# A column block of the attention weights is turned by VectorE and DMAs instead of TensorE

## The chip, the cores and the metric

The kernel runs on one core of a Trainium2 chip. The metric is device time in microseconds, from the program's start to its end. A core has a matrix engine (TensorE, PE in the profile; its weight loads are PEld), a vector engine (VectorE, DVE), an engine for activations (ScalarE, ACT), a general engine (GpSimd, POOL) and one that mostly issues DMAs (SyncE, SP). Each runs its own queue of instructions in order; semaphores make one wait for another. Results of TensorE go to a small memory, PSUM, and are copied from there to the main on-chip memory, SBUF, by VectorE or ScalarE.

## The reference

There are 32 graphs of 512 nodes with 64 features each and one normalized adjacency matrix for all. Four layers follow each other, each with a layer norm before it and a residual sum behind it. The change concerns the fourth, which takes most of the time:

```python
def gat_layer(x, graph, W, b):
    h = x @ W
    s = jnp.einsum('bnd,bmd->bnm', h, h) * graph
    s = jnp.where(s == 0.0, NEG_INF, s)
    a = jax.nn.softmax(s, axis=2)
    return jnp.einsum('bnm,bmd->bnd', a, h) + b
heads = jax.vmap(lambda W, b: gat_layer(flow_x, graph, W, b))(Wh, bh)   # 8 heads, 128 wide
x = jax.nn.leaky_relu(cat, negative_slope=0.01)                          # heads side by side
out = gat_layer(x, graph, W_out, b_out)                                  # 64 wide
return jax.nn.leaky_relu(out, negative_slope=0.01)
```

All is float32. The softmax is taken along rows, and the product with the values sums over the columns, so the weights have to be transposed between the two: TensorE sums over the partition axis, which holds rows after the softmax and has to hold columns for the product.

## The kernel before

The first three layers take the first 470 us or so. Then comes the attention stage, `run`, which the change touches. Its piece of work is a **unit** (`Pair`): two heads of one graph (`Heads`, 128 units) or the output layer of two graphs (`Out`, 16 units). A unit's weights p_att hold, for each of its two members k, 512 rows as four groups r of 128 partitions, by 512 columns as four blocks j of 128.

The stage goes in **slots**, four to a unit, and the order in each slot is written out by hand (`slot(k)`, in a manual schedule) for TensorE, VectorE and ScalarE. What a unit does is given by its offset from its first slot:

- offset -1 to 2: the scores of row group r (L387), 0 to 3: the softmax's front (`soft`): s_att on VectorE (L373), the exponentials p_att on ScalarE (L366);
- offset TR = 5 to 8: the transposes of block j (L400), 16 of them for each block, into two PSUM buffers pt_ps for the lower and upper half of the rows. ScalarE copies one half to pt_att (L406), VectorE the other (L408);
- offset VA = 6 to 9: the values av of block j (L415), which accumulate over the four blocks;
- offset 5, on VectorE at the end of the slot: `recips`, the reciprocal of the row sums and a small transpose; SyncE then writes them to DRAM (rec_row, L430) and reads them back as rows (recb, L435);
- offset END = 9: `normalize` (L444), av times recb, and after it the projection of the heads (y_ps, L527), cat (L535), and leaky (L312).

Units overlap. The slot in which one unit has offset 9 is the slot in which the next has offset 5, so in VectorE's order of that slot the normalize of one unit stands ahead of recips of the next: s_att twice, normalize, the pt_att copy, recips.

Every fourth head unit (a new graph) has one more chain: VectorE makes hn at the end of one slot (L475 to L479), GpSimd makes hs of it in two operations (L484), TensorE transposes hs in the next slot (hx_ps, L291), and ScalarE copies that to hx, from which the scores' operand g comes (g_ps, L509). In the nine units that belong to two graphs, eight slots also hold a product gT_ps (L566) for the output layer.

Pools matter in three places: pt_ps, y_ps, g_ps, hx_ps and gT_ps share three PSUM buffers, the scores have two, p_att has two. GpSimd and SyncE are not in the manual schedule; their orders follow that of the program.

Of the kernel before, what the change touches and what calls it, by code (L numbers as in the profile page):

```python
# [8 lines left out]
F32 = mybir.dt.float32  # L9
# [5 lines left out]
P = 128  # L15
# [7 lines left out]
def fast_form(  # L23
# [25 lines left out]
    nc = tc.nc  # L49
    B, N, F = x.shape  # L50
    C = N // P
    H, _, D = w_heads.shape
    G = min(8, B)
    NG = B // G
    F2 = 2 * F

    const = ctx.enter_context(tc.tile_pool(name="const", bufs=1))
    xpool = ctx.enter_context(tc.tile_pool(name="xpool", bufs=1))
# [30 lines left out]
    def load_blockdiag(src, name):  # L89
        t = setup.tile([P, F2], F32, name=name)  # L90
        nc.vector.memset(t, 0.0)
        for k in range(2):
            nc.gpsimd.dma_start(t[k * F : (k + 1) * F, k * F : (k + 1) * F], src)
        return t
# [34 lines left out]

    wgT2 = setup.tile([P, F2], F32, name="wgT2")  # L130
    bh = const.tile([P, H], F32, name="bh")
# [74 lines left out]
    def halves(k):  # L206
        return slice(k * F, (k + 1) * F)
# [8 lines left out]
    def acc(name, shape):  # L216
        return acc_of[0].tile(shape, F32, name=name, tag=acc_of[1])
# [22 lines left out]
    def gat_weights():  # L240
        pw = acc("wgT_ps", [P, F2])
        nc.tensor.transpose(pw, wg2, ident)
        nc.scalar.copy(wgT2, pw)
        pa = acc("wa_ps", [P, 2])
        nc.tensor.matmul(pa, lhsT=wg2, rhs=a12, start=True, stop=True)
        wa = setup.tile([P, 2], F32, name="wa")
        nc.scalar.copy(wa, pa)
        nc.vector.memset(wa2, 0.0)
        for k in range(2):
            nc.vector.tensor_copy(wa2[halves(k), k : k + 1], wa[halves(k), 1:2])  # L250
        nc.vector.memset(wa1, 1.0)
        size = tiny.tile([P, 2], F32, name="size")
        nc.vector.scalar_tensor_tensor(size, wa, -1.0, wa, op0=OP.mult, op1=OP.max)

        pz = acc("size_ps", [P, 2])
        nc.tensor.matmul(pz, lhsT=wa1, rhs=size, start=True, stop=True)
        nc.vector.tensor_scalar(
            sound[:, :2], pz, 2 * E_MAX, None, op0=OP.is_le
        )
        nc.vector.tensor_scalar(wa1, wa1, wa[:, 0:1], None, op0=OP.mult)  # L260
# [39 lines left out]
    TR = C + 1  # L300
# [13 lines left out]
    class Pair:  # L314
# [4 lines left out]

        def begin(self):
            self.p = pbuf.tile([P, 2, C, N], F32, name="p_att")
            self.sum = tiny.tile([P, 2, C], F32, name="sum_att")
            self.negmax = tiny.tile([P, 2, C], F32, name="negmax")
            self.pts = {}
# [55 lines left out]
        def scores(self, r):  # L382
# [3 lines left out]
            for k in range(2):  # L386
# [2 lines left out]
                    start=True, stop=True,  # L389
                )  # L390

        def transpose(self, j):
            pt = pbuf.tile([P, 2, N], F32, name="pt_att", bufs=2)
            self.pts[j] = [pt[:, k] for k in range(2)]

            ps = [ps_m.tile([P, 2, C, F], F32, name="pt_ps", tag="m") for half in range(2)]
            for k in range(2):
                for r in range(C):
                    for half in range(2):
                        nc.tensor.transpose(  # L400
                            ps[half][:, k, r],
                            self.p[halves(half), k, r, j * P : (j + 1) * P],
                            ident[halves(half), halves(half)],
                        )
            pth = pt.rearrange("p k (r half q) -> p k r half q", r=C, half=2)
            nc.scalar.copy(pth[:, :, :, 0, :], ps[0])  # L406

            return lambda: nc.vector.tensor_copy(pth[:, :, :, 1, :], ps[1])  # L408

# [218 lines left out]
    with (  # L628
# [92 lines left out]
        def project(terms, tag):  # L721
            p = ps_o.tile([P, C, 2, F], F32, name=tag, tag="po")
            for c in range(C):
                for i, (t, w) in enumerate(terms):
                    nc.tensor.matmul(  # L725
                        p[:, c],
                        lhsT=t[:, c * P : (c + 1) * P],
                        rhs=w,
                        start=(i == 0),
                        stop=(i == len(terms) - 1),  # L730
                    )
            return p
# [104 lines left out]
        def slot(k):  # L837
# [50 lines left out]
            if l1:  # L888
                po = project([(nt1, wl2[0])], "po1a")
                z = work.tile([P, C, F2], F32, name="z")  # L890
                nc.scalar.activation(z, po.rearrange("p c b f -> p c (b f)"), AF.Relu)
# [60 lines left out]
    wk = ctx.enter_context(tc.tile_pool(name="work_b", bufs=2))  # L952
# [9 lines left out]
    def run(units, products):  # L962
        units = units + [None] * 4

        def at(k, off, span=C):

            for u in range(len(units)):
                if units[u] and 0 <= k - u * C - off < span:
                    yield units[u], k - u * C - off

        exps = []

        def led_in(k):
            for u, j in at(k, -3 * C, 3 * C + END + 5):
                if u.leads(j - 3 * C):
                    yield u, j - 3 * C

        def slot(k):
            for u, r in at(k, -1):
                u.scores(r)  # L980

            led = list(led_in(k))
            for u, off in led:
                u.row_halves(off)

            while exps:
                exps.pop(0)()

            copies = []

            def transposes():
                for u, j in at(k, TR):
                    copies.append(u.transpose(j))

            if not led:
                transposes()
            for u, j in at(k, VA):
                u.values(j)  # L1000
            for u, j in at(k, VA - 1, 1):
                u.make_v()
            for n, u in products:
                u.product(k - n * C)
            for u, j in at(k, -3 * C, 3 * C):
                u.prep_pe(j - 2 * C)
            if led:
                transposes()
            for u, j in at(k, END, 5):
                u.end_pe(j)  # L1010

            def mid():
                for u, j in at(k, END, 1):
                    u.normalize()

            now = list(at(k, 0))
            for u, r in now:
                exps.append(u.soft(r, mid))
            if not list(led_in(k + 1)):
                while exps:  # L1020
                    exps.pop(0)()
            if not now:
                mid()
            for copy in copies:
                copy()
            for u, j in at(k, END, 5):
                u.end_late(j)
            for u, j in at(k, TR, 1):
                u.recips()
            for u, j in at(k, -3 * C, 3 * C):  # L1030
                u.prep_late(j - 2 * C)

        with tc.manual_schedule(
            engines={
                mybir.EngineType.PE,
                mybir.EngineType.DVE,
                mybir.EngineType.Activation,
            }
        ):
            for k in range(-3 * C, len(units) * C):  # L1040
                slot(k)
# [56 lines left out]
def general_form(  # L1098
# [27 lines left out]
    NG = B // G  # L1126
    F2 = 2 * F

# [18 lines left out]
    def load_blockdiag(src, name):  # L1147
        t = const.tile([P, F2], F32, name=name)
        nc.vector.memset(t, 0.0)
        for k in range(2):  # L1150
            nc.gpsimd.dma_start(t[k * F : (k + 1) * F, k * F : (k + 1) * F], src)
        return t
# [462 lines left out]
def gnn_stack_kernel(tc: tile.TileContext, *args: bass.AP):  # L1615
    nc = tc.nc
    with tc.tile_pool(name="flag", bufs=1) as pool:
        again = pool.tile([1, 1], mybir.dt.int32, name="again")
        fast_form(tc, *args, again)
        with tc.If(nc.values_load(again[0:1, 0:1])):  # L1620
            general_form(tc, *args)
# [35 lines left out]
```

## Time and profile before

| | before |
|---|---|
| time, median of 3 runs | 2357.64 us (2357.25 to 2358.01) |
| span of the profiled run | 2359.7 us |
| one of the exponentials, L366 | 723 ns, 1152 of them |
| one s_att, L373 | 680 ns, 1152 |
| pt_att copy on VectorE, L408 / ScalarE, L406 | 687 / 581 ns, 576 each |
| one transpose instruction, L400 | 226 ns, 9216, overlapping |
| DMAs in the attention stage | 24 GB/s, all from SyncE |
| DMAs issued by GpSimd | only in the first 15 us |

Instructions overlap in an engine's pipeline, so a mean times a count is more than the engine's busy time. The chain of waits goes back from the last instruction, at each step to what released it; its shares say which engine the end waited for. A group's idle time names who ended it. In the lists in order of time, the first number is the start in microseconds from the span's start, the second the duration.

### The profile page before, as it was taken

Reading aid. Unit: us, or ns where it says so; the run is one execution under the profiler, and the core shown is the slowest. Engines: PE = TensorE matmul, PEld = TensorE weight load, DVE = VectorE, ACT = ScalarE, POOL = GpSimd, SP = SyncE. Lnnn points to the kernel's source line nnn. Section 1 sums busy time; section 2 is a strip of 40 time slices with the busy share of each in tenths; the row PEclk is TensorE's granted clock in tenths of the full one; section 3 lists DMA queues with packets and bytes.
Section 4 is the critical chain, followed back from the end, with each engine's and each line's share of the span. In section 5 each row is a group of like instructions: output and inputs, shape, how many; then the busy total and the mean of one; then the engine's idle time right before and its main releaser. Section 6 shows DMA issues by size and latency. Waiting matters only on the chain.

```text
span 2359.7 us, 46961 instructions
## 1 busy us (share of the span) xinstructions
PE 2259.6 (96%) x17786; PEld 1107.3 (47%) x17786; DVE 1792.1 (76%) x4350; ACT 1583.2 (67%) x3660; POOL 68.0 (3%) x104
## 2 busy tenths in 40 slices
PE   7999999689999999999999999999999999999997
PEld 4677777634444444444444444444444444444443
DVE  5788878577777777777777777777777787878776
ACT  3444443277777777777777777777777777778775
POOL 2000000000000000000000000000000000000000
PEclk9999999589999999999999999999999999999999
DMA  3000000000000000000000000000000000000001
GB/s 106 1 1 1 1 1 1 0 15 24 20 28 21 27 24 24 28 20 28 22 26 24 24 24 24 24 24 24 24 24 26 22 29 19 24 19 24 20 24 38
DMA packets 44059, 51.89 MB, mean 22 GB/s; under 512 B 15864, under 2 KB 25248, under 8 KB 43696
## 3 DMA queue, kind: packets, MB, share of 16 engines
q1 hardware_dynamic: 43312, 48.60, 6.6%
q8 instruction: 142, 2.33, 0.4%
q0 software_dynamic: 512, 0.20, 0.1%
q14 instruction: 93, 0.76, 0.1%
HBM read 43.98 MB, written 4.78 MB: 21 GB/s over the span
## 4 chain that ended last, share of the span: by engine, by line
PE 89%; DVE 6%; POOL 2%; ACT 1%; issue 1%; DMA 1%; SPq 0%; POOLq 0%; DVEq 0%; ACTq 0%
PE s_ps L387 23%; PE av L415 22%; PE pt_ps L400 13%; PE nt_ps L706 7%; PE acc L789 6%; PE gT_ps L566 5%; PE y_ps L527 5%; PE g_ps L509 2%; DVE pt_att L408 2%; POOL hs L484 2%; PE po L725 1%; PE hx_ps L291 1%; PE e_ps L753 1%; PE po1a L725 1%; PE wh L725 1%
## 5 line engine op out<-in xcount | busy, mean ns | idle before, releaser
L366 ACT ACTIVATE p_att<-s_att,negmax 128x512 f32<-128x512 f32 x1152 | 827.6, 723 | 0.0
L373 DVE CUSTOM_DVE_ANT_0 s_att<-s_ps,flow_neg 128x512 f32<-128x512 f32 x1152 | 739.9, 680 | 5.3 <-PE s_ps L387 5.2
L408 DVE COPY pt_att<-pt_ps 128x512 f32<-128x512 f32 x576 | 395.6, 687 | 281.0 <-PE pt_ps L400 223.7
L387 PE MATMUL s_ps<-hx,g 64*128 64x512 f32 x2048 | 571.0, 636 | 5.8 <-DVE negmax L373 5.1
L415 PE MATMUL av<-pt_att,hn 128*64 128x512 f32 x2048 | 552.4, 618 | 0.0
L400 PEld LDWEIGHTS pt_ps<-ident,p_att 64*128 64x128 f32 x9216 | 373.6, 138 | 374.1 <-issue 227.7
L406 ACT COPY pt_att<-pt_ps 128x512 f32<-128x512 f32 x576 | 334.6, 581 | 156.6 <-PE pt_ps L400 150.7
L400 PE MATMUL pt_ps<-ident,p_att 64*128 64x64 f32 x9216 | 415.2, 226 | 2.3 <-ACT pt_att L406 0.8
L535 ACT ACTIVATE cat<-y_ps,bh 128x512 f32<-128x512 f32 x256 | 162.0, 684 | 168.4 <-PE y_ps L527 168.4
L387 PEld LDWEIGHTS s_ps<-hx,g 64*128 64x128 f32 x2048 | 156.5, 188 | 245.7 <-DVE negmax L373 178.3
L366 ACT ACTIVATION_READ_ACCUMULATOR p_att<-s_att,negmax 128x1 f32 x1152 | 224.5, 195 | 0.0
L444 DVE TENSOR_TENSOR o_att<-av,recb 128x512 f32<-128x512 f32 x144 | 99.6, 691 | 140.5 <-PE av L415 140.5
L415 PEld LDWEIGHTS av<-pt_att,hn 128*64 128x64 f32 x2048 | 101.4, 135 | 156.7 <-PE s_ps L387 86.4
L312 DVE SCALAR_TENSOR_TENSOR cat<-cat 128x1024 f32<-128x1024 f32 x128 | 155.6, 1215 | 0.0
L789 PE MATMUL acc<-v,s 128*128 128x65 f32 x1024 | 136.5, 301 | 10.3 <-DVE s L779 10.3
L789 PEld LDWEIGHTS acc<-v,s 128*128 128x128 f32 x1024 | 134.8, 217 | 13.5 <-issue 12.3
L527 PE MATMUL y_ps<-o_att,wh_sb 64*128 64x512 f32 x512 | 131.7, 591 | 0.0
L566 PE MATMUL gT_ps<-cat,wo_sb 128*64 128x512 f32 x512 | 131.7, 593 | 0.0
L521 ACT COPY g<-g_ps 128x512 f32<-128x512 f32 x128 | 68.7, 589 | 84.8 <-PE g_ps L509 84.8
L706 PE MATMUL nt_ps<-adj_t,hn 128*128 128x512 f32 x256 | 115.9, 596 | 0.8 <-DVE hn L670 0.8
L373 DVE DVE_READ_ACCUMULATOR2_ANT negmax<- 128x1 f32 x1152 | 95.6, 83 | 0.0
L387 PE MATMUL s_ps<-gs 64*128 64x512 f32 x256 | 72.3, 641 | 24.2 <-DVE gs L584 24.2
(169 smaller groups left out, 1603.1 us busy)
## 6 DMA issues: line engine op xcount, KB each, us to landing
recb<-rec_row SPq DMA_DIRECT2D x288, 128.0 KB
rec_row<-rect SPq DMA_DIRECT2D x576, 1.0 KB
out_dram<-y SPq DMA_DIRECT2D x32, 128.0 KB
x<-in_x_dram SPq DMA_DIRECT2D x3, 1024.0 KB
x<-in_x_dram SPq DMA_DIRECT2D x4, 256.0 KB
adj_raw<-in_adj_dram SPq DMA_DIRECT2D x1, 1024.0 KB
wh_sb<-in_L_gnn_Wh_dram SPq DMA_DIRECT2D x2, 256.0 KB
wo_sb<-in_L_gnn_W_out_dram SPq DMA_DIRECT2D x1, 256.0 KB
```

What stands on the lines that cost most here:

```text
L366: nc.scalar.activation(self.p[:, k, r, :], ns[:, k], AF.Exp, bias=self.negmax[:, k, r : r + 1], scale=-1.0, accum_out=self.sum[:, k, r : r ...
L373: nc.vector.tensor_tensor_reduce(out=ns[:, k], in0=ps[:, k], in1=flow_neg[:, r], scale=-1.0, scalar=BIG, op0=OP.add, op1=OP.min, accum_out ...
L387: nc.tensor.matmul(ps[:, k], lhsT=g[halves(k), r * P : (r + 1) * P], rhs=x[halves(k), :], start=True, stop=True,)
L400: nc.tensor.transpose(ps[half][:, k, r], self.p[halves(half), k, r, j * P : (j + 1) * P], ident[halves(half), halves(half)],)
L406: nc.scalar.copy(pth[:, :, :, 0, :], ps[0])
L408: return lambda: nc.vector.tensor_copy(pth[:, :, :, 1, :], ps[1])
L415: nc.tensor.matmul(self.av[halves(k), :], lhsT=self.v(k, j), rhs=pt[k], start=(j == 0), stop=(j == C - 1),)
L527: nc.tensor.matmul(ps, lhsT=wh_sb[halves(k), h, :], rhs=self.o[halves(k), :], start=True, stop=True,)
L535: nc.scalar.activation(self.cat[:, k], pss[k], AF.Identity, bias=bh[:, h : h + 1], scale=1.0)
L566: nc.tensor.matmul(self.gps[halves(k), :], lhsT=wo_sb[:, h, :], rhs=Heads.cat[b + k, h], start=(h == 0), stop=(h == H - 1),)
L706: nc.tensor.matmul(p, lhsT=lhs(k), rhs=adj_t[:, k, :], start=(k == 0), stop=(k == C - 1))
L789: nc.tensor.matmul(acc[:, r], lhsT=self.s[k][j // 2][:, j % 2, r * P : (r + 1) * P], rhs=self.v[:, k, j], start=(j == 0), stop=(j == C - 1),)
```

## The change

The transpose of the last of the four column blocks leaves TensorE. At offset 5, after `recips` and so behind VectorE's other work of that slot, the new `route` has VectorE transpose the 32 by 32 pieces of block 3 inside their quarter of the partitions, with one instruction for each of the two members. The pieces then lie in the right orientation but, except for those on the diagonal, in the wrong quarter of the partitions. Sixteen DMAs of 32 partitions by 1 KB move them from `turn` to `turned`: the four on the diagonal from SyncE, the other twelve from GpSimd. The values of block 3 at offset 9 read `turned`. Both new buffers are double.

With the blocks that stay on TensorE, the second copy goes to ScalarE for blocks 0 and 2 and stays on VectorE for block 1, so ScalarE now has five of the six copies of a unit. It is meant to take work from TensorE and copies from VectorE.

```diff
+        def route(self, j):
+            t = wk.tile([P, Q, 2, C, 32], F32, name="turn")
+            for k in range(2):
+                nc.vector.transpose(
+                    t[:, :, k].rearrange("p a r i -> p r a i"),
+                    self.p[:, k, :, j * P : (j + 1) * P].rearrange(
+                        "p r (a i) -> p r a i", i=32
+                    ),
+                )
+            pt = wk.tile([P, Q, 2, C, 32], F32, name="turned")
+            for b in range(Q):
+                for a in range(Q):
+                    (nc.sync if a == b else nc.gpsimd).dma_start(
+                        pt[a * 32 : (a + 1) * 32, b], t[b * 32 : (b + 1) * 32, a]
+                    )
+            self.pts[j] = [pt[:, :, k].rearrange("p b r q -> p r b q") for k in range(2)]
...
             nc.scalar.copy(pth[:, :, :, 0, :], ps[0])
+            if j != 1:
+                nc.scalar.copy(pth[:, :, :, 1, :], ps[1])
+                return None
 
             return lambda: nc.vector.tensor_copy(pth[:, :, :, 1, :], ps[1])
...
             def transposes():
-                for u, j in at(k, TR):
+                for u, j in at(k, TR, C - 1):
                     copies.append(u.transpose(j))
...
             for copy in copies:
-                copy()
+                if copy:
+                    copy()
...
             for u, j in at(k, TR, 1):
                 u.recips()
+                u.route(C - 1)
```

## The prediction

> **What bounds the kernel now.** I read the shares first, then the chain of waits, then busy time by stretch, then one stretch in order of time.
>
> ```profile
> PE 2259.6 (96%) x17786; PEld 1107.3 (47%) x17786; DVE 1792.1 (76%) x4350; ACT 1583.2 (67%) x3660; POOL 68.0 (3%) x104
> ...
> PE 89%; DVE 6%; POOL 2%; ACT 1%; issue 1%; DMA 1%; SPq 0%; POOLq 0%; DVEq 0%; ACTq 0%
> PE s_ps L387 23%; PE av L415 22%; PE pt_ps L400 13%; PE nt_ps L706 7%; PE acc L789 6%; PE gT_ps L566 5%; PE y_ps L527 5%; PE g_ps L509 2%; DVE pt_att L408 2%; POOL hs L484 2%; PE po L725 1%; PE hx_ps L291 1%; PE e_ps L753 1%; PE po1a L725 1%; PE wh L725 1%
> ```
>
> TensorE sets the time, and the transposes (L400) are 13% of the chain: 0.13 x 2359.7 / 576 column blocks = 0.53 us a block. The one GpSimd item is hs, 2%, although POOL is busy for 3%: the chain passes through it.
>
> ```profile
> 1000.00:1500.00 500.00, 488.58 (x4116) 210.29 (x4116) 385.27 (x975) 374.83 (x899) 10.65 (x18) 1.00 0.08 25
> ```
>
> That is the busy time by stretch (length, then PE, PEld, DVE, ACT, POOL, clock, DMA share, GB/s) in the attention stage: PE 98%, DVE 77%, ACT 75%.
>
> The issues of rec_row on SyncE come once a unit, so their starts give the units' periods. From 1485.58 us they are 13.3, 11.3, 14.9, 14.7, 13.7, 13.3, 11.9 and 12.2 us; hs returns every 116.5 us (1440.62 to 1557.10), so a cycle is nine units and the ninth takes 11.3. Sixteen cycles are 1864 us. The two units of 13.3 are those with hs in them. The chain through one of them:
>
> ```profile
> 1550.73 1.01 PE av L415 x4
> 1551.74 1.06 PE s_ps L387 x4
> 1552.80 0.86 PE y_ps L527 x4
> 1553.66 1.01 PE av L415 x4
> 1554.67 0.69 PE pt_ps L400 x16
> ...
> 1556.14 0.34 DVE hn L475
> ...
> 1556.51 0.43 DVE hn L476
> ...
> 1557.10 1.20 POOL hs L484 x2
> ...
> 1558.34 0.65 PE hx_ps L291 x4
> ```
>
> From the end of a unit's last values (1551.74) to hx_ps is 6.60 us, and TensorE waits about 0.5 us for hs; from hx_ps to the next unit's last values (ending at 1565.02) it is 6.7.
>
> **What the Trainium skill says.** "DMA: Bandwidth & Descriptors", section "Anatomy of one DMA": a GpSimd DMA costs about 2.0 us plus bytes / 436e3, mostly the wait for the write's receipt. Before has such DMAs only in its start, from HBM beside the big loads, where they landed after 4.6 to 8.1 us; no SBUF to SBUF one is in the trace. "SBUF — State Buffer", section "Who interferes with whom": a VectorE instruction outside the two-port modes with at most one SBUF input does not hold up GpSimd. The stage's copies (687 ns for 512 elements from PSUM) and leaky (1215 for 1024) run at about one element a cycle, so I charge no starvation of descriptors. "TensorE: Matmul & The Clock Gate", Part 1: a whole idle window of about 3.4 us halves the clock. The slices of before agree in kind: 0.5 from 405 to 485 us, where TensorE has gaps of 5 to 10 us.
>
> **The change part by part.**
>
> TensorE: 16 transposes a unit go, 0.53 us. Times 144 units: -77 us if nothing else comes to bind.
>
> ScalarE: two more copies (blocks 0 and 2), one fewer (block 3): +0.58 us a unit (581 ns, L406). From 374.83/500 x 12.95 = 9.7 us a unit to 10.3, against 12.4 that TensorE would need: off the path. I charge nothing; the work hiding it is TensorE's.
>
> VectorE: three of four copies go (3 x 687 = 2.06 us), two transposes of 128x512 come. Before shows only STREAM_TRANSPOSE of 128x32 at 211 ns; other operations of 512 elements take 680 to 690. Bounds 0.68 and, at half that rate, 1.3; I take 0.72, paced 0.65. In total VectorE does less, but the new work stands behind normalize and recips of its slot, and normalize waits for the previous unit's last values.
>
> GpSimd: 12 DMAs a unit. Start-up shows the cost of one:
>
> ```profile
> L93 POOL DMA_DIRECT2D ws<-n_L_gnn_weight_self_dram x2 | 1.1, 543 | 0.0
> ...
> L117 POOL DMA_DIRECT2D b_out<-in_L_gnn_b_out_dram x2 | 1.1, 533 | 0.0
> ...
> L104 POOL DMA_DIRECT2D bias_b<-in_L_gnn_bias_dram x1 | 0.8, 756 | 0.4 <-issue 0.4
> L126 POOL DMA_DIRECT2D bh_raw<-in_L_gnn_bh_dram x1 | 0.5, 542 | 0.0
> ```
>
> 64 rows, 64 rows of one element, 128 rows, 8 rows: fixed cost, little with rows. I take 0.53; bounds 0.50 and 0.756. Twelve take 6.4 us. In the built program each waits for the landing of the one eight before it (8 x 0.53 = 4.2 us earlier), which costs nothing at a landing of 2.5 us. Behind them in GpSimd's queue stand the two hs operations (in every fourth head unit the order is 12 DMAs, hs, hs), and for hs waits hx_ps, in order on TensorE.
>
> SyncE: 4 more issues, 0.32 us each by rec_row's pace (1.29 for four), ahead of recb. recb starts 1.3 us later and has some 6 us in hand; the four land before GpSimd's twelve. Nothing. The 0.5 MB a unit over 12 us is 43 GB/s beside 24 now, and q1 takes 6.6% of the DMA engines for 48.6 MB: no bound.
>
> **The new loop.** Time 0 is the end of a unit's last values. normalize, reciprocal and the small transpose: 1.05 (their records after 1551.74, less the copy of block 0 that leaves VectorE). Two transposes: to 2.4. First DMA at 2.5, the twelfth starts at 2.5 + 11 x 0.53 = 8.3. Landing 2.5 after its start (bounds 2.0, the skill's fixed cost, and 4.6): 10.8. TensorE's waits for twelve semaphores 0.2 (my guess), values 1.08: the period can't be under 12.1 us.
>
> **hs.** The twelfth is issued at 8.9, hs ends at 10.1, hx_ps starts at 10.15 instead of 6.60: +3.55, less the 0.53 removed: +3.0.
>
> By cycle: two hs units +6.0; the short ones 11.3, 11.3, 11.9, 12.2 go to 12.1: +1.7; the three long ones (14.9, 14.7, 13.7) stay bound by TensorE and gain 0.53 each: -1.6. Sum +6.1, times 16: +98 us. The idle gap at hx_ps is about 4.0 us; a free-running window of 3.4 fits whole into it in some (4.0 - 3.4)/3.4, about one in five, and costs some 2 us: 32 x 0.2 x 2 = +12. 2357.6 + 98 + 12 = **2468 us**.
>
> **Rivals.**
> - *TensorE stays the bound, all DMAs hidden*: 2357.6 - 77 = 2281. For it: 98% busy, three slots between the turn and its use. Against: twelve issues at the start-up price leave hs late whatever the landing. It needs issues under about 0.35 us, which no row shows. 0.07; half hidden, around 2330, another 0.04.
> - *The gain and the two waits cancel*: 2358, with issues of about 0.4 us. 0.02.
> - *GpSimd is dearer than start-up shows*. At 0.756 an issue: loop 2.5 + 11 x 0.756 + 2.5 + 1.3 = 14.6 for all seven units without hs (+12.7 a cycle), hs units +5.7 each: +24 x 16 = 385, 2740. At 0.53 but landing 4.6: the ninth waits 0.4, loop 14.6, hs units +3.4: +19 x 16 = 310, 2668. For it: 4.6 is the least landing measured. Against: those read HBM beside megabyte loads. 0.24, most of it below 2680.
> - *VectorE's longer slot holds scores up*: scores of the slot after next need the score buffer read by then. s_att ends near 3.95, TensorE asks at 3.6: 0.4 us, which lies inside the waits above. Slow transposes (1.3) would shift route, hs and loop by 1.2: two hs units +2.4, four short ones +4.8, times 16, +115: 2580, inside the range.
> - *ScalarE becomes the bound*: 10.3 of 12 us; 0.01.
>
> **How the numbers follow.** Forecast (both waits on GpSimd, 2400 to 2560) 0.62; dearer GpSimd 0.25 with the ScalarE case; cancelled 0.02; faster 0.11. The range, 2365 to 2680, leaves out the faster cases (0.11) and the top of the dear one (some 0.07). Faster 0.11, same 0.02, slower 0.87.
>
> **What would show it.** Right: the chain's share of GpSimd and DMA grows from 3% to above 15%, PE's busy share falls to about 88% (2259.6 - 77 of 2468), TensorE's waits before av name DMAs in the short units, before hx_ps name hs at some 4 us, pt_ps falls to 6912 instructions. Wrong if: DMA_DIRECT2D on POOL is well under 0.4 us, hs runs within 1 us of hn, or units without hs are shorter than 11 us.

## The result, and the profile after

The changed kernel takes 2578.64 us (median of 4 runs, 2577.62 to 2579.96), the kernel before 2357.82 in the same comparison: ratio 1.0928, 95% interval 1.0913 to 1.0944, 221 us slower. The forecast had the direction and both waits, and half of the amount: 2468 us, so 110 us of the 221.

Shares and costliest groups of the changed kernel's page (busy us, mean ns of one | idle time of the engine just before them, and what ended most of it):

```profile
PE 2262.9 (88%) x15482; PEld 1042.4 (40%) x15482; DVE 1714.4 (67%) x4206; ACT 1645.2 (64%) x3804; POOL 914.1 (35%) x1832
...
L407 POOL DMA_DIRECT2D turned<-turn x1728 | 845.4, 497 | 1354.6 <-issue 654.0
L390 PE MATMUL s_ps<-hx,g 64*128 64x512 f32 x2048 | 609.2, 674 | 45.2 <-DVE negmax L376 44.5
...
L398 DVE STREAM_TRANSPOSE turn<-p_att 128x512 f32<-128x512 f32 x288 | 187.9, 690 | 52.6 <-issue 46.9
...
L292 PE MATMUL hx_ps<-ident,hs 128*128 128x128 f32 x128 | 29.7, 373 | 123.3 <-POOL hs L507 122.5
...
turned<-turn POOLq DMA_DIRECT2D x1728, 32.0 KB, 2.1
```

All engines but GpSimd have lost share, so the time is in waits. The last line's 2.1 us is the median from issue to landing. TensorE's waits in the attention stage, 490 to 2560 us (total us, times, longest):

```profile
PE hx_ps L292 <- POOL hs L507: 122.5, 31, 6.7
PE av L438 <- DMA turned<-turn: 53.4, 42, 3.6
PE s_ps L390 <- DVE negmax L376: 44.1, 76, 1.8
```

The same view of before, over its attention stage, has none for `turned` and for the other two:

```profile
PE hx_ps L291 <- POOL hs L484: 14.3, 31, 0.8
PE s_ps L387 <- DVE negmax L373: 4.8, 13, 0.4
```

These three waits therefore grew by 201 us, of 213 by which TensorE's idle time grew (span less PE busy: 2575.7 - 2262.9 = 312.8, against 2359.7 - 2259.6 = 100.1).

The surprise is in PE's busy time. With 77 us of transposes gone it should be 2183; it is 2263. The attention stage as one stretch, of before (columns as in the prediction):

```profile
490.00:2345.00 1855.00, 1809.33 (x15296) 778.63 (x15292) 1421.88 (x3586) 1388.41 (x3325) 36.69 (x62) 1.00 0.08 24
```

And of the changed kernel:

```profile
490.00:2560.00 2070.00, 1814.28 (x13017) 714.79 (x13014) 1346.68 (x3447) 1451.15 (x3470) 882.79 (x1790) 0.96 0.21 58
```

The clock fell from 1.00 to 0.96: fewer instructions, slower in the mean. Over the span the mean clock went from 0.981 to 0.948. As an estimate that counts idle time too, what the clock takes away is (1 - clock) times the span: 0.052 x 2575.7 = 134 us against 0.019 x 2359.7 = 45, so 89 us more. The span's difference adds up as -77 (transposes) + 80 (slower matmuls) + 213 (idle) = 216.

By units (starts of rec_row), a typical cycle went from 13.3 11.3 14.9 14.7 13.7 13.3 11.9 12.2 11.3 (116.6) to **18.1 12.1 14.2 14.2 13.1 18.2 12.0 12.7 12.0** (126.6): +10 x 16 = 160 us. The other 61 are stray longer units. A unit with hs, in order of time (start, length, [idle before]):

```profile
1541.97 1.08 PE L438 MATMUL av<-turned,hn 128*64 128x512 f32 x4
...
1544.50 1.30 DVE L398 STREAM_TRANSPOSE turn<-p_att 128x512 f32<-128x512 f32 x2 [0.36 <-issue]
...
1546.34 5.85 POOL L407 DMA_DIRECT2D turned<-turn  x12 [7.23 <-DMA rec_row<-rect]
...
1547.97 0.43 DVE L499 SCALAR_TENSOR_TENSOR hn<-hn,rstd 128x256 f32<-128x256 f32 x1
...
1552.21 1.19 POOL L507 TENSOR_TENSOR hs<-hn,root_d 128x256 f32<-128x256 f32 x2
1553.46 1.11 PE L292 MATMUL hx_ps<-ident,hs 128*128 128x128 f32 x4 [3.76 <-POOL hs L507]
1554.50 2.08 PE L390 MATMUL s_ps<-hx,g 64*128 64x512 f32 x4
1556.37 1.92 PE L532 MATMUL g_ps<-hx,m 64*128 64x512 f32 x4
```

hn has been ready since 1548.40 (1547.97 + 0.43), hs starts the moment the twelfth issue ends, and hx_ps starts 10.5 us after the last values' end (1542.98). Then the matmuls run at half speed: the scores take 2.08 us for the 1.13 they take at full clock, g_ps 1.92 for 1.02. With hx_ps itself (1.11 for 0.65) that is 2.3 us.

### The profile page after: what moved, and what is told of

It is laid out like the page before. It is cut to its first block, busy times and chain, and to the rows that moved or that the text cites. A ratio compares the mean times of both kernels' runs of the same rounds, so it can differ in the third digit from the quotient of the medians.

```text
span 2575.7 us, 46612 instructions
## 1 busy us (share of the span) xinstructions
PE 2262.9 (88%) x15482; PEld 1042.4 (40%) x15482; DVE 1714.4 (67%) x4206; ACT 1645.2 (64%) x3804; POOL 914.1 (35%) x1832
## 3 DMA queue, kind: packets, MB, share of 16 engines
q8 instruction: 127, 2.08, 0.4%
## 5 line engine op out<-in xcount | busy, mean ns | idle before, releaser
L407 POOL DMA_DIRECT2D turned<-turn x1728 | 845.4, 497 | 1354.6 <-issue 654.0
L390 PE MATMUL s_ps<-hx,g 64*128 64x512 f32 x2048 | 609.2, 674 | 45.2 <-DVE negmax L376 44.5
L438 PE MATMUL av<-pt_att,hn 128*64 128x512 f32 x1536 | 419.9, 625 | 0.0
L420 PEld LDWEIGHTS pt_ps<-ident,p_att 64*128 64x128 f32 x6912 | 277.5, 139 | 270.5 <-issue 187.0
L426 ACT COPY pt_att<-pt_ps 128x512 f32<-128x512 f32 x432 | 251.1, 581 | 143.2 <-PE pt_ps L420 143.0
L420 PE MATMUL pt_ps<-ident,p_att 64*128 64x64 f32 x6912 | 299.4, 225 | 1.2 <-ACT pt_att L426 0.6
L398 DVE STREAM_TRANSPOSE turn<-p_att 128x512 f32<-128x512 f32 x288 | 187.9, 690 | 52.6 <-issue 46.9
L438 PE MATMUL av<-turned,hn 128*64 128x512 f32 x512 | 141.6, 628 | 44.1 <-DMA turned<-turn 38.7
L428 ACT COPY pt_att<-pt_ps 128x512 f32<-128x512 f32 x288 | 170.9, 593 | 0.0
L438 PEld LDWEIGHTS av<-pt_att,hn 128*64 128x64 f32 x1536 | 77.2, 137 | 210.1 <-issue 108.1
L812 PEld LDWEIGHTS acc<-v,s 128*128 128x128 f32 x1024 | 134.9, 217 | 13.5 <-issue 12.3
L292 PE MATMUL hx_ps<-ident,hs 128*128 128x128 f32 x128 | 29.7, 373 | 123.3 <-POOL hs L507 122.5
```

What stands on the lines that cost most here:

```text
L390: nc.tensor.matmul(ps[:, k], lhsT=g[halves(k), r * P : (r + 1) * P], rhs=x[halves(k), :], start=True, stop=True,)
L398: nc.vector.transpose(t[:, :, k].rearrange("p a r i -> p r a i"), self.p[:, k, :, j * P : (j + 1) * P].rearrange("p r (a i) -> p r a i", i ...
L407: (nc.sync if a == b else nc.gpsimd).dma_start(pt[a * 32 : (a + 1) * 32, b], t[b * 32 : (b + 1) * 32, a])
L420: nc.tensor.transpose(ps[half][:, k, r], self.p[halves(half), k, r, j * P : (j + 1) * P], ident[halves(half), halves(half)],)
L428: nc.scalar.copy(pth[:, :, :, 1, :], ps[1])
L438: nc.tensor.matmul(self.av[halves(k), :], lhsT=self.v(k, j), rhs=pt[k], start=(j == 0), stop=(j == C - 1),)
```

## The experiments

Before, in these comparisons, took 2359 to 2360 us (medians). Each kernel starts from the changed one unless its edit says otherwise. e3 and e4 leave the move between partitions out of what the values read.

### The two waits, one at a time

**e1**: hs on VectorE, so nothing of TensorE's stands behind the issues.

```diff
-                    nc.gpsimd.tensor_tensor(
+                    nc.vector.tensor_tensor(
```

> The change, with hs made by VectorE (L507: nc.vector instead of nc.gpsimd) so that it no longer stands behind the twelve DMAs in GpSimd's queue. Theory (the queue in front of hs is the main cost, and the half clock follows from that gap): TensorE's wait before hx_ps falls from 3.8 us to under 1, the units with hs fall from 18.1 to about 13, the clock of the stage goes back to about 0.99; 32 x 5 = 160 us less, 2420 (2380 to 2450). Rival (the wait for the DMAs' landing in every unit is the main cost): only the hx_ps wait goes, 32 x 2 = 60 us or less, 2520 or more.

Measured: 2413.52 us, ratio 1.0234 (1.0217 to 1.0251), 165 us less than the changed kernel. TensorE's waits in its attention stage:

```profile
PE av L438 <- DMA turned<-turn: 57.5, 41, 4.0
...
PE hx_ps L292 <- DVE hs L507: 1.6, 6, 0.4
```

The waits for hs are gone, the hs units are mostly back at 13.2 to 13.7, the mean clock is 0.975. The short units mostly stay at 11.7 to 12.7, and the waits before av for `turned` stay too (53.4 us in the changed kernel).

**e3**: all DMAs issued, but the values read `turn`, so none waits for a landing.

```diff
-            self.pts[j] = [pt[:, :, k].rearrange(...) for k in range(2)]
+            self.pts[j] = [t[:, :, k].rearrange(...) for k in range(2)]
```

> The change, with the sixteen DMAs issued as before but the values of block 3 reading turn instead of turned, so that TensorE doesn't wait for any landing (this leaves the move between partitions out of the result). Theory: hs units stay at 17 to 18 us, the short units fall from 12.0 to about 11: 4 a cycle x 1 us x 16 = 64, with the stray late landings up to 90: 2500 (2480 to 2540). Rival (landing is the main cost): below 2420.

Measured: 2509.73 us, 1.0641 (1.0623 to 1.0658). The hs units take 19.0 us at the median (18.2 in the changed kernel), and the clock is the lowest with e10's, 0.943.

**e4**: the same without the 16 DMAs.

```diff
-            pt = wk.tile(...)
-            for b in range(Q): ...dma_start(...)
```

> The change without its sixteen DMAs: VectorE turns block 3, and the values of block 3 read turn (this leaves the move between partitions out of the result). What is left is TensorE's saving, the new copies and VectorE's longer slot. Theory: TensorE stays the bound and 144 x 0.53 = 77 us are gained, less up to 0.4 us for scores behind VectorE in the short units (4 of 9 of 144, 25 us): 2290 (2275 to 2310). Rival (ScalarE's copies or VectorE's slot cost as much as they save): 2340 or more.

Measured: 2285.16 us, 0.9693 (0.9676 to 0.9709). Its typical cycle is 12.7 10.8 14.2 14.2 13.1 12.7 11.4 12.2 10.8. Its page:

```profile
PE 2176.7 (95%) x15482; PEld 1012.3 (44%) x15482; DVE 1700.8 (75%) x4206; ACT 1644.4 (72%) x3804; POOL 67.9 (3%) x104
```

This is the gain that was hoped for: 74 us of 77, with the new transposes and copies in place. So the whole loss is in the DMAs. Added to e4, DMAs that nobody reads cost 2510 - 2285 = 225 us, some 200 of them in the hs units (32 x 6.3, from 12.7 to 19.0), so mostly by the queue in front of hs; reading what they bring costs 69 more. From the other side, e1 puts the loop at 2414 - 2285 = 128 us and hs at 165. The two overlap, so neither split is a property of one wait alone; the queue is the larger part either way.

### The clock

**e2**: two unneeded matmuls into hx_ps ahead of its transposes, so that half of TensorE's gap is filled.

```diff
+                for _ in range(2):
+                    nc.tensor.matmul(pt, lhsT=ident, rhs=urow, start=True, stop=True)
```

> The change, with two matmuls of ident by urow (128x512 each) into hx_ps just ahead of the transposes of hs, whose results are overwritten: 2 us of added TensorE work in the gap of 3.8 us in each of 32 units, hs as late as before. Theory (the gap halves the clock afterwards, and that costs about 2.3 us a time): no idle window is long enough, scores and g after hx_ps go back from 2.08 and 1.92 to 1.13 and 1.02 us, 32 x 2.3 = 70 us less: 2505 (2490 to 2530). Rival (the slow matmuls come from something else, such as the DMAs' traffic): same or slower, 2575 to 2640.

Measured: 2539.77 us, 1.0758 (1.0735 to 1.0781): 39 us less, for more work, where 70 had been expected. Mean clock 0.966. The filling didn't always help. Two units with the same wait, in order of time:

```profile
1145.92 0.66 PE L521 MATMUL hx_ps<-ident,hs 128*128 128x128 f32 x4 [1.85 <-POOL hs L507]
1146.51 1.13 PE L390 MATMUL s_ps<-hx,g 64*128 64x512 f32 x4
...
1273.40 0.66 PE L521 MATMUL hx_ps<-ident,hs 128*128 128x128 f32 x4 [1.85 <-POOL hs L507]
1273.99 2.02 PE L390 MATMUL s_ps<-hx,g 64*128 64x512 f32 x4
```

Behind a wait of 1.85 to 1.87 us the next matmuls were slow in 10 cases of 19; behind the six waits for hs of 1.47 to 1.61 us never (nor behind one of 2.27). In the changed kernel all 31 waits for hs are 2.9 us or more, and all 31 were followed by slow matmuls.

So the length of a gap doesn't decide alone. The traces hold a record of the granted clock, and in each run all its changes are whole multiples of 3.41 us apart: time is cut into fixed windows. Here are some of them (columns as above), first two of e2 around each of the two waits, then three of the changed kernel around the wait that ended at 1553.46:

```profile
1144.38:1147.80 3.42, 1.88 (x10) 1.10 (x12) 0.52 (x3) 1.18 (x3) 1.47 (x3) 1.00 0.17 55
1147.80:1151.21 3.41, 3.41 (x30) 1.38 (x28) 1.31 (x4) 2.80 (x9) 0.00 (x0) 1.00 0.00 0
...
1270.68:1274.09 3.41, 1.56 (x9) 0.56 (x7) 1.69 (x5) 0.00 (x0) 2.65 (x6) 1.00 0.34 93
1274.09:1277.50 3.41, 3.41 (x8) 1.04 (x8) 1.31 (x4) 1.30 (x3) 0.00 (x0) 0.50 0.01 2
...
1548.17:1551.58 3.41, 1.52 (x22) 0.57 (x16) 3.38 (x8) 1.67 (x4) 3.41 (x8) 1.00 0.56 161
1551.58:1555.00 3.42, 1.54 (x6) 1.21 (x8) 0.85 (x4) 0.39 (x1) 1.81 (x4) 0.50 0.14 37
1555.00:1558.41 3.41, 3.41 (x10) 0.88 (x9) 1.31 (x4) 1.00 (x4) 0.00 (x0) 0.50 0.00 0
```

The wait that ended at 1273.40 lay wholly in one window, which left TensorE busy for 1.56 us of 3.41 (0.46); the one that ended at 1145.92 began in the window before, and its own kept 1.88 (0.55). Over the attention stages of all 14 traces (from 495 us to 25 us before the end), every one of the 134 windows at full clock in which TensorE was busy for less than 0.42 was followed by a window at half clock, 24 of the 41 between 0.42 and 0.50, and none of the 7350 above. "TensorE: Matmul & The Clock Gate", Part 1, of the Trainium skill has the clock fall after an idle window of about 3.4 us. The length of the window agrees with these traces; that it must be idle does not, and the measurement decides. A wait of 3.76 us, the usual one for hs, has at least half of itself, 1.88 us or 0.55 of a window, in one window or the next: wherever it lies, it leaves a window that is busy for 0.45 at the most, and all 31 brought the clock down.

### Undoing the lateness

**e5**: `route` one slot earlier, in a loop of its own.

```diff
             for u, j in at(k, TR, 1):
                 u.recips()
-                u.route(C - 1)
+            for u, j in at(k, TR - 1, 1):
+                u.route(C - 1)
```

> The change with route a slot earlier: at offset 4 behind s_att, where it doesn't stand behind the previous unit's normalize; hs stays on GpSimd, the sixteen DMAs stay as they are. Theory (both costs are the place of the twelve DMAs in time: a loop from one unit's last values over normalize, route and twelve issues to the next unit's, and hs behind the issues): with route some 4 us earlier the last landing has about 3 us in hand and the issues end before hn is ready, so units without hs come to 10.8 to 11.4 in the short ones and those with hs to 12.7 to 13.3: 2300 (2285 to 2330), below the kernel before. Rival (the twelve DMAs and their landing cost as such, wherever they start): 2400 or more.

Measured: **2303.44 us, 0.9764 (0.9748 to 0.978)**, faster than before. GpSimd's queue and VectorE's hn, in order of time, then two waits of TensorE:

```profile
1561.05 5.88 POOL L407 DMA_DIRECT2D turned<-turn  x12 [4.57 <-issue]
...
1566.89 0.43 DVE L499 SCALAR_TENSOR_TENSOR hn<-hn,rstd 128x256 f32<-128x256 f32 x1
...
1567.47 1.18 POOL L507 TENSOR_TENSOR hs<-hn,root_d 128x256 f32<-128x256 f32 x2 [0.54 <-DVE hn L499]
...
PE hx_ps L292 <- POOL hs L507: 18.8, 31, 3.3
...
PE av L438 <- DMA turned<-turn: 1.6, 1, 1.6
```

The issues cost what they did, but they end at 1566.93, before hn (1567.32), so hs waits for hn again. The waits for hs fall from 122.5 to 18.8 us, those for `turned` from 53.4 to 1.6, the typical cycle is 13.1 10.7 14.2 14.2 13.1 13.1 11.0 11.7 10.6. Lateness, not the number of DMAs, was nearly all of the cost: e5 is 18 us above e4. Of these 18, three hs units of 17.3 to 17.4 us instead of 13.1 make 12.7; in each of them a pause in GpSimd's issues (see the stray units below) falls into the batch in front of hs.

**e6**: e5 with hs on VectorE as in e1.

> As e5_route_early, with hs on VectorE as well. Theory: nothing is left for it to gain, within 10 us of e5 (it adds 0.85 us of VectorE in 32 slots and takes 0.35 us off the way to hx_ps). If hs still stood behind issues in e5, this one is 30 us or more below it.

Measured: 2301.84 us, 0.9753 (0.9736 to 0.9769), no different from e5. Two things cancel: the three long hs units are gone, and the other hs units take 13.5 us instead of 13.1, some 11 us together.

### Fewer issues on GpSimd

**e7**: e1 with eight DMAs each for SyncE and GpSimd.

```diff
-                    (nc.sync if a == b else nc.gpsimd).dma_start(
+                    (nc.sync if (a + b) % 2 == 0 else nc.gpsimd).dma_start(
```

> The change with hs on VectorE and the sixteen DMAs split evenly, eight on SyncE and eight on GpSimd, instead of four and twelve. Theory (the loop's length is issues times 0.49 us plus the landing): the loop shortens by 4 x 0.49 = 2.0 us from 11.9, under TensorE's 10.8, so of the 128 us between e1 and e4 most go: 2310 (2295 to 2350). Against it: SyncE's issue takes 0.58, and recb stands behind it. Rival (landing, not issue): 2390 or more.

Measured: 2405.28 us, 1.0194 (1.0177 to 1.0211), only 8 us less than e1, where some 100 had been expected. SyncE's queue:

```profile
1698.48 1.28 SPq L453 DMA_DIRECT2D rec_row<-rect  x4
1700.19 2.42 SPq L407 DMA_DIRECT2D turned<-turn  x4
1702.77 1.11 SPq L458 DMA_DIRECT2D recb<-rec_row  x2
1703.93 2.50 SPq L407 DMA_DIRECT2D turned<-turn  x4
```

SyncE now is the late one: its last issue ends 1706.43 - 1698.48 = 7.95 us after rec_row's start, and in the changed kernel GpSimd's ended 1552.19 - 1544.17 = 8.0 after it.

**e9**: e7 with recb issued a slot later, so that it doesn't stand between the eight.

```diff
+            for u, j in at(k, TR + 1, 1):
+                u.recips_back()
```

> As e7 (hs on VectorE, eight DMAs each), with the loads of recb issued a slot later, so that all eight of SyncE's moves stand ahead of them; in e7 recb stood between the fourth and the fifth, and the last issue was no earlier than GpSimd's twelfth in e1. Theory (issues make the loop's length): last issue some 2 us earlier, landing before TensorE asks in the short units: 2325 (2300 to 2350). If recb now comes too late for normalize instead: up to 2390. Rival (landing of 2.1 us or the DMAs' number as such): 2400 as e7.

Measured: 2396.2 us, 1.0145 (1.0125 to 1.0165): a miss, 9 us less instead of 80. VectorE's and TensorE's waits from 500 to 2400 us:

```profile
DVE o_att L471 <- DMA recb<-rec_row: 112.9, 42, 5.9
...
PE av L438 <- DMA turned<-turn: 11.6, 8, 3.5
```

The wait before av fell from 53.7 us in e7 to 11.6, as meant; but recb now lands too late for normalize, which in e7 never waited for it. The wait was moved.

**e12**: e5 with the split and the late recb of e9.

> As e5, with eight DMAs each on SyncE and GpSimd, recb's loads a slot later, hs on GpSimd. GpSimd paused 2.3 to 2.9 us after every 121 issues in the change, e1 and e5; eight a unit instead of twelve make 9 or 10 pauses of 14. Theory: a few of the 18 us between e5 and e4 go: 2295 (2287 to 2303), pauses again 121 issues apart. Rival (the pauses follow time or other traffic): as many as in e5. If recb is late for normalize: 2310 or more.

Measured: 2304.45 us, 0.9764 (0.9747 to 0.9781), the same as e5, where a few us less had been expected. Nobody waits there for `turned`, so issuing it in less time is worth nothing. No pause delays hs here, but nine units now take 111.8 to 113.1 us instead of 111.6, and that takes the gain back.

### The copies

**e8**: the kernel before with the change's rule for the copies (blocks 0, 2 and 3 wholly on ScalarE), nothing else.

> The kernel before with the change's rule for the copies alone: blocks 0, 2 and 3 have both copies on ScalarE, block 1 one on each (seven of eight on ScalarE); nothing else of the change. Theory (ScalarE has room): 2358, within 15 us. Rival (ScalarE's copies hold up the PSUM buffers of the transposes): 2390 or more.

Measured: 2358.55 us, 0.9996 (0.9987 to 1.0005): no difference. **e10** is the changed kernel, **e11** is e5, with the second copies of blocks 0 and 2 back on VectorE:

```diff
-            if j != 1:
-                nc.scalar.copy(pth[:, :, :, 1, :], ps[1])
-                return None
```

> The change with the second copy of blocks 0 and 2 back on VectorE. Theory of the loop: block 0's copy stands between normalize and recips, 0.6 us on the way from one unit's last values to the DMAs and to hs: six of nine units (four short ones, two with hs) 0.6 us longer, 6 x 0.6 x 16 = 58: 2637 (2605 to 2660). Rival (VectorE isn't on the loop, only GpSimd): 2565 to 2595.

> As e5 (route a slot earlier), with the second copy of blocks 0 and 2 back on VectorE. Theory: with the loop gone TensorE sets the pace and the place of the copies is worth little: 2303 within 15 us. Rival (VectorE's fuller slots hold up the scores): 2325 or more, and then the copies are a part of the change that pays.

Measured: e10 2661.82 us (1.1277, 1.1257 to 1.1297), 83 more than the changed kernel, where 58 had been expected; e11 2332.53 (0.9886, 0.9868 to 0.9903), 29 more than e5, where nothing had been expected of it. In e10 TensorE's waits for negmax before the scores rise to 99 us (42 in the changed kernel over the same 500 to 2400 us), and in e11 to 27.5 (7.8 in e5, to 2260 us). With the new transposes in VectorE's queue these copies make it late for the scores; without them (e8) it has room for the copies. So the copies' part of the change is worth having, and only beside the rest.

## Why the prediction was right in direction and low in size

The measured 2579 lies above the 2400 to 2560 that the forecast gave to its own mechanism. The stated range holds it only because it left room up to 2680 for dearer issues and late landings, which did not come about; that was luck.

- **TensorE, -77 us.** Right: e4 gained 74, and the long units of the changed kernel are shorter by 0.7, 0.5 and 0.6 for the 0.53 put down.
- **ScalarE off the path, at nothing.** Right by e8.
- **VectorE's transposes, 0.72, paced 0.65.** Right: 690 ns, two in 1.30.
- **GpSimd, 0.53 an issue.** Right: 497 ns, twelve in 5.85 us for 6.4. The dearer cases (0.756, or a landing of 4.6 as the rule) didn't come about; in the first of them the seven units without hs go from 90.0 to 7 x 14.6 = 102.2, which is +12.2 and not +12.7, some 8 us in all. "SBUF — State Buffer", section "Who interferes with whom", on which I charged no starvation, agrees: 496 ns at the least and the median, 558 at the most, beside VectorE at work.
- **Landing 2.5.** Right: median 2.1 (1.6 to 4.6), near the 2.0 of "DMA: Bandwidth & Descriptors", section "Anatomy of one DMA".
- **First DMA at 2.5 us.** Too early: it is at 3.36 (1546.34 - 1542.98, where the next scores take over TensorE). VectorE stood idle 0.36 before the transposes, and 0.54 passed between their end (1545.80) and the first issue. The cheaper issues make up for most: the twelfth ends at 9.2 for 8.9.
- **The loop, 12.1.** Right: two batches in a row start 11.83 or 11.84 us apart (1577.07 less 1565.23, 1601.66 less 1589.83), and the short units are 12.0 to 12.7.
- **SyncE, 0.32 an issue.** Wrong: rec_row's pace doesn't hold for these; 582 ns at the median, four in 2.46. It cost nothing here, since GpSimd was later, and it set the end in e7.
- **Scores held up by VectorE, 0.4 us, "inside the waits above".** The size is right (0.44 us in the unit around 1547), and they add up to 44 us. That they lie inside the others wasn't shown: no run took them away alone. Nor do they come from the longer slot as such: e4, with the transposes and without DMAs, has 12 us of them, e3, with DMAs that nobody reads, 48. With the DMAs VectorE also stands idle for 46.9 us ahead of the transposes, for nothing that the profile shows (L398 in the page above), and in e4 for 0.7.
- **hs.** The queue was right: hx_ps at 10.48 for 10.15, a gap of 3.76 for about 4.0. **The step that failed is what follows it**: "one in five, and costs some 2 us: 32 x 0.2 x 2 = +12". The 2 us were right (2.3); the one in five was wrong. It was all 31, because no window has to be idle as a whole: one that is busy for less than about 0.45 is enough, and a wait of 3.76 us leaves such a window wherever it lies ("The clock" above). The hs units went to 18.1 instead of 16.3: 1.8 x 32 = 58 us more than "two hs units +6.0", 12 of which the forecast had.
- **Not foreseen: the stray units**, some 61 us. In GpSimd's queue a pause of 2.3 to 3.1 us recurs every 121 DMAs, in all eleven runs that issue them and whatever the time between. One of them in e1, in order of time:

```profile
1945.62 0.98 POOL L407 DMA_DIRECT2D turned<-turn  x2 [7.46 <-PE y_ps L550]
...
1949.42 4.88 POOL L407 DMA_DIRECT2D turned<-turn  x10 [2.82 <-issue]
```

In e1 the next values wait 3.09 us for it and run slowly (1.97 us for four matmuls that take 1.08), so one pause also costs a stretch at half clock. The spacing is the same in e5 and e12, where most pauses fall into slack. In the changed kernel twelve of the fourteen pauses fall into units that are 1.5 to 3.9 us longer than the typical ones, 35 us together, and e4, without DMAs, has no such units; e6 has the pauses and no such units, since nothing waits for them there. So the pauses account for more than half of the 61 us. The rest is not accounted for unit by unit, and the cause of the pauses stays open.

Sum: 98 forecast for the two waits, 58 at the hs units and 61 for stray units make 217 of the 221. Two of the prediction's own signs do less than they seemed to. PE's share of 88% came out right for a wrong reason: 2263 of 2576, with half-clock time in it, instead of 2183 of 2468. And the chain of waits of the changed kernel breaks off near the end of the program, with 0% for every engine, so the 15% couldn't be read.

## What to carry to other kernels

An engine's DMA issues are work in its queue: twelve of them are 6 us in which nothing else of that engine starts, and what must be counted is who stands behind them, not only when the data lands. Price a gap in TensorE with the slow matmuls after it: here 3.8 us of waiting cost about 6, and two waits of 1.85 us cost different amounts by where they lay. Before giving up such a change, ask whether its start is late by necessity: its input was ready a slot earlier, and the same 16 DMAs issued then (e5) turn +9.3% into -2.4%.

## What the runs showed of the hardware

- In these traces the clock changes only at the borders of windows of 3.41 us. Full clock was followed by half clock behind every window with TensorE busy for less than 0.42 of it (134 of 134), and behind none with more than 0.50 (0 of 7350). At half clock, every window busy for less than 0.84 was followed by another at half clock (57 of 57), and every one busy for more than 0.88 by full clock (157 of 157).
- So gaps of 1.85 to 1.87 us before hx_ps brought the clock down about half of the time, and those of 2.9 us and more every time; slow matmuls then lasted 3 to 5 us.
- GpSimd pauses 2.3 to 3.1 us after each 121 DMAs it issues.
- Issues of SBUF to SBUF DMAs of 32 partitions by 1 KB took 0.50 us on GpSimd and 0.58 on SyncE, against 0.32 for rec_row's on SyncE.
